# Attention kernel: the score maxima of later units dealt out to the steps by a plan made at build time

## The chip, the cores and the metric

The kernel runs on one core of a Trainium2 chip. The metric is the device time of one execution in microseconds; lower is better. The times of before come from three runs, and one further execution was profiled.

## The reference

Four layers with residuals on 4096 rows of 256 numbers: attention a, a soft mixture of experts, attention b, the same mixture again. Only the attentions matter here. Each has 16 heads of 16 columns and is causal:

```
x = x + attention_a(layernorm(x))       # has a bias bo and a term exp(denom_bias) in the denominator
x = x + experts(layernorm(x))
x = x + attention_b(layernorm(x))
x = x + experts(layernorm(x))

sim  = q @ k^T / 4 per head, masked above the diagonal
e    = exp(sim - max(sim, axis=-1))
attn = e / (sum(e) + exp(denom_bias));  out = (attn @ v) @ Wo^T + bo
```

The row maximum of all scores has to be known before the first exponential of that row.

## The kernel before

**Units and steps.** The queries are cut into 8 blocks of 512 rows, the heads into 4 groups of 4. A unit is one group g of one block b; the 32 units run in the order of `units`, block by block. Two passes are made over a unit's keys.

The first pass, `steps_a(u)`, finds the row maxima. It is a generator, and each of its turns is called a piece here: TensorE writes scores (queries as weights) into two PSUM banks called `bank`, and VectorE takes one maximum from each bank (L410; near the diagonal L431, L444 and L454). A unit of block b has 8b + 5 pieces, so an attention has 1056. The banks come from `net.bank()`, a ring of three (`at_psa`). After a unit's last piece `finish_a` reduces the maxima to one number a row and head (`ng`, L465), splits and transposes it on VectorE (`nt`, L473), and sends it over DRAM into the tile `qm` (two kinds of DMA on SyncE's queue, L475 and L478). The first piece of a key tile loads the next tile (`load_to`, L374; a query tile at L367), into a ring of 11 key tiles and 4 query tiles.

The second pass, `steps_b(u)`, has 4(b + 1) steps for a unit, one for each 128 keys; 576 for an attention. A step has two halves (two heads each): score matmuls (`sc<-q,k`), matmuls that subtract the maxima (`sc<-qm,one`, they need `qm`), and an exponential on ScalarE (L533). The last four steps of a unit lie on the diagonal and are 512, 384, 256 and 128 columns wide; GpSimd masks them (L537). A step's product with the values, `weigh` (`o<-pb,va`), is made one step later. After a unit's last one ScalarE copies `o` (L501) and `epilogue` begins.

**What else is put into the steps.** `net.beside(2)` is called once in each step, between two portions of its pieces: it counts two, starts what has become due, and then runs one item, of `urgent` first, else of `side`. In blocks 0 to 3 `side` holds the 16 items of `pieces(b + 4)`, begun with the block's first step: two with transposes (items 3 and 8), four projections to queries and keys (10 to 13: four matmuls into a `bank`, a copy on ScalarE L173, a subtraction on VectorE L174, DMAs to DRAM) and two projections to values (14 and 15). The epilogue's parts fall due 6, 8, 4 and 8 counts after one another: the denominators' reciprocal on VectorE (L558, L559), the division on GpSimd (L571), the fetch of the block's output, and two output projections (`project`, added to x on VectorE at L601), which are `urgent`.

**The order.** Every matmul is kept in program order, so the loop at the end of `run` sets TensorE's order: in each step the two halves' scores, then half of the step's pieces, then `beside`, then the values' product of the step before, then the other pieces. How many pieces a step gets is asked of `wanted(n)`, n counting half steps: unit u's pieces lie evenly between the due time of unit u - 1's pieces and its own, and they are due 8 half steps (10 early on) before the unit's second pass begins:

```
due = [0] + [max(0, e - (10 if e <= 32 else 8)) for e in ends[:-1]]
...
return first + -(-(ends_a[u] - first) * (n - lo) // (hi - lo))
```

In the profile, `bank`, `sc` and `o` are TensorE's outputs, all recorded at the helper's line L68.

Of the kernel before, what the change touches and what calls it, by code (L numbers as in the profile page):

```python
# [24 lines left out]
NQB = S // QB  # L25
# [3 lines left out]
NG = H // HG  # L29
# [14 lines left out]
class _Net:  # L44
# [28 lines left out]
    def bank(self):  # L73
        return self.banks.tile([P, 512], F32, name="bank")
# [32 lines left out]
class _Attention:  # L107
# [158 lines left out]
    def dense_values(self, b, psb=None):  # L266
        bank = (lambda: self.front(psb)) if psb else self.net.bank
        return [lambda t2=t2: self.values(b, t2, bank()) for t2 in range(2)]

    def run(self, ready, experts):  # L270

# [4 lines left out]
        with ExitStack() as ctx:  # L276
# [13 lines left out]
            before = [cp.tile([P, P], F32R, name=f"before{n}") for n in range(2)]  # L290
            behind = cp.tile([P, half], F32R, name="behind")
            for n in range(3):
                w = P if n < 2 else half
                f = net.ep.tile([P, QB], F32, name="ot", bufs=3)[:, 0:w]
                for h2 in range(2):
# [3 lines left out]
                        out=fh, in_=fh, compare_op=ALU.is_ge, fill=1.0 if n < 2 else NEG,  # L299
# [12 lines left out]
            for p in range(2):  # L312
                f = net.ep.tile([P, QB], F32, name="ot", bufs=3)[:, 0:P]
                nc.gpsimd.memset(f, 0.0)
                for h2 in range(2):
                    for l in range(2):
                        nc.gpsimd.affine_select(
                            out=f, in_=f, compare_op=ALU.not_equal, fill=1.0,
# [28 lines left out]
            pairs = deque([psb])  # L347

            def third():
                actx.close()  # L350
                pairs.extend([psb, pool("psc", 1, space=PSUM)])
                net.banks = pool("psx", 1, space=PSUM)

            ks, qs, qms = {}, {}, {}
            units = [(g, b) for b in range(NQB) for g in range(NG)]


            kseq = [(u, kb) for u, (g, b) in enumerate(units) for kb in range(b + 1)]
# [145 lines left out]
            def values_to(n):  # L504
                while len(queue) > n:
                    weigh(queue.popleft())
# [99 lines left out]

            ends, ends_a, total = [], [], 0
            for g, b in units:  # L610
                ends.append(8 * (b + 1) + (ends[-1] if ends else 0))
                total += 8 * b + 5
                ends_a.append(total)

            due = [0] + [max(0, e - (10 if e <= 32 else 8)) for e in ends[:-1]]
            runs = iter(f for u in range(len(units)) for f in steps_a(u))
            done_a = [0]

            def maxima_to(n):
                while done_a[0] < min(n, total):  # L620
                    next(runs)
                    done_a[0] += 1

            def wanted(n):
                for u in range(len(units)):
                    if due[u] > n:
                        lo, hi = due[u - 1], due[u]
                        first = ends_a[u - 1]
                        return first + -(-(ends_a[u] - first) * (n - lo) // (hi - lo))
                return total  # L630

            front = []
            if ready:
# [15 lines left out]
                front += self.dense(b, psb, prp)  # L649
            for f in front:  # L650
                f()
                maxima_to(min(done_a[0] + 1, wanted(0)))
            maxima_to(wanted(0))
            n = 0
            for u, (g, b) in enumerate(units):
                if g == 0 and 4 <= b + 4 < NQB:
                    net.side.extend(self.pieces(b + 4))
                if g == 0 and b == NQB - 1:
                    experts.load()

                last = deque()
                if u == len(units) - 1:
                    last.extend(experts.ahead())
                    third()
                for p, _ in enumerate(steps_b(u)):
                    n += 1
                    if last and p % 4 == 3 and p >= 8 * (b + 1) - 4 * len(last):
                        last.popleft()()
                    if p % 2 == 0:
                        continue  # L670
                    while (
                        g >= 2 and net.side and u + 2 < len(units)
                        and units[u + 2][1] > max(3, b)
                    ):
                        net.beside()
                    want = wanted(n + 1)
                    maxima_to((done_a[0] + want) // 2)
                    net.beside(2)
                    values_to(1)
                    maxima_to(want)  # L680
# [622 lines left out]
```

## Time and profile before

| | us |
|---|---|
| median of three runs (5069.66 to 5073.91) | 5070.28 |
| the profiled execution, and its span | 5074.49, 5072.8 |
| first attention's steps, in the span | 86.2 to 1753.7 |
| second attention's steps | 2619.1 to 4289.3 |
| TensorE busy, share of the span | 4938.9, 97% |
| VectorE busy | 4087.2, 81% |
| ScalarE busy | 2631.4, 52% |

In a line of the timeline stand the start, the time, the engine, the line of the code, the operation with its tiles and shapes, how many instructions were merged (x2), and in brackets the engine's idle time before them and what ended it. In a group's line stand the count, the busy time and the mean in ns of one, and after the second bar the engine's idle time just before them. In a line of the stages stand the stretch, its length, the busy time of TensorE, its weight loads, VectorE, ScalarE and GpSimd with the number of instructions, the granted TensorE clock, and the DMA engines' share and rate. A line of the waits names who waited for whom: total us, times, longest.

### The profile page before, as it was taken

Reading aid. Unit: us, or ns where it says so; the run is one execution under the profiler, and the core shown is the slowest. Engines: PE = TensorE matmul, PEld = TensorE weight load, DVE = VectorE, ACT = ScalarE, POOL = GpSimd, SP = SyncE. Lnnn points to the kernel's source line nnn. Section 1 sums busy time; section 2 is a strip of 40 time slices with the busy share of each in tenths; the row PEclk is TensorE's granted clock in tenths of the full one; section 3 lists DMA queues with packets and bytes.
Section 4 is the critical chain, followed back from the end, with each engine's and each line's share of the span. In section 5 each row is a group of like instructions: output and inputs, shape, how many; then the busy total and the mean of one; then the engine's idle time right before and its main releaser. Section 6 shows DMA issues by size and latency. Waiting matters only on the chain.

```text
span 5072.8 us, 79746 instructions
## 1 busy us (share of the span) xinstructions
PE 4938.9 (97%) x31216; PEld 2706.8 (53%) x31216; DVE 4087.2 (81%) x6392; ACT 2631.4 (52%) x3112; POOL 1175.7 (23%) x1178
## 2 busy tenths in 40 slices
PE   7999999999999999999989999999999999999999
PEld 4555455555455444458855555555554554444588
DVE  5688989898988378887757888898989883888877
ACT  4566666766667721223235666667666677212222
POOL 3211100000000155554422111000000001555454
PEclk9999999999999999999999999999999999999999
DMA  7433222221111013443454332222211210134443
GB/s 261 147 113 126 76 67 70 65 67 63 57 63 57 33 73 113 146 143 122 147 186 147 115 126 75 66 70 62 70 63 58 63 57 33 75 113 146 144 146 111
DMA packets 266442, 499.20 MB, mean 98 GB/s; under 512 B 44976, under 2 KB 110000, under 8 KB 258384
## 3 DMA queue, kind: packets, MB, share of 16 engines
q1 hardware_dynamic: 260832, 485.57, 28.8%
q10 hardware_dynamic: 4896, 7.87, 0.5%
q8 instruction: 245, 4.01, 0.3%
q14 instruction: 133, 1.09, 0.1%
q0 software_dynamic: 336, 0.66, 0.0%
HBM read 336.73 MB, written 156.76 MB: 97 GB/s over the span
## 4 chain that ended last, share of the span: by engine, by line
PE 86%; DVE 8%; DMA 2%; ACT 2%; issue 1%; POOL 1%; SPq 0%; ACTq 0%; POOLq 0%; DVEq 0%
PE o L68 27%; PE bank L68 21%; PE sc L68 18%; PE acc L68 9%; PE lg L68 8%; DVE mx L410 4%; PE ps L71 2%; ACT pb L533 1%; PE bank L71 0%; DVE lT L1013 0%; DVE mx L454 0%; DMA d<-ot 0%; DMA rb<-dd 0%; ACT L533 0%; DMA l<-ld 0%
## 5 line engine op out<-in xcount | busy, mean ns | idle before, releaser
L533 ACT ACTIVATE pb<-sc 128x1024 f32<-128x1024 f32 (+3 forms) x2304 | 2070.1, 951 | 1080.4 <-PE sc L68 1077.6
L410 DVE TENSOR_REDUCE mx<-bank 128x1 f32<-128x512 f32 x3584 | 2223.2, 682 | 236.6 <-PE bank L68 231.3
L68 PE MATMUL bank<-k,q 64*128 64x512 f32 (+3 forms) x5376 | 1222.3, 413 | 50.8 <-DVE mx L410 23.3
L68 PEld LDWEIGHTS bank<-k,q 64*128 64x128 f32 x5376 | 659.1, 185 | 1022.8 <-DVE mx L410 735.1
L68 PE MATMUL o<-pb,va 128*32 128x512 f32 (+3 forms) x9216 | 1154.2, 571 | 1.6 <-ACT ot L501 1.3
L68 PE MATMUL sc<-q,k 64*128 64x512 f32 (+3 forms) x4608 | 941.6, 386 | 11.2 <-ACT pb L533 11.1
L68 PE MATMUL sc<-qm,one 64*128 64x512 f32 (+3 forms) x4608 | 915.4, 376 | 0.0
L68 PEld LDWEIGHTS sc<-q,k 64*128 64x128 f32 x4608 | 477.7, 186 | 138.0 <-issue 50.9
L68 PEld LDWEIGHTS sc<-qm,one 64*128 64x128 f32 x4608 | 488.7, 186 | 71.5
L757 ACT ACTIVATE e<-e 128x1024 f32<-128x1024 f32 x126 | 133.3, 1058 | 651.9 <-POOL e L756 651.9
L68 PE MATMUL acc<-e,x 128*128 128x512 f32 x1008 | 461.7, 602 | 9.1 <-POOL e L764 9.1
L68 PE MATMUL o<-ys,lT 128*128 128x256 f32 x2048 | 459.0, 381 | 0.0
L68 PE MATMUL lg<-zone,xnT 128*128 128x512 f32 x1008 | 453.1, 592 | 1.2 <-ACT xnT L1036 1.2
L68 PEld LDWEIGHTS o<-ys,lT 128*128 128x128 f32 x2048 | 385.4, 191 | 56.7 <-issue 7.0
L537 POOL TENSOR_SCALAR_AFFINE_SELECT pb<-pb 128x256 f32<-128x256 f32 x512 | 204.8, 406 | 839.3 <-ACT pb L533 832.3
L68 PEld LDWEIGHTS o<-pb,va 128*32 128x32 f32 x9216 | 183.1, 108 | 312.3 <-issue 282.4
L955 POOL TENSOR_TENSOR e<-l,mc 128x1024 f32<-128x1024 f32 x120 | 281.2, 2365 | 284.6 <-DMA l<-ld 186.8
L756 POOL TENSOR_TENSOR e<-l,m 128x1024 f32<-128x1024 f32 x126 | 240.9, 1912 | 423.7 <-DVE m L755 419.2
L68 PEld LDWEIGHTS acc<-e,x 128*128 128x128 f32 x1008 | 190.5, 192 | 245.4 <-issue 229.8
L388 POOL MEMSET mx<- 128x192 f32 x64 | 16.3, 259 | 1312.0 <-DVE ng L465 1292.3
L68 PEld LDWEIGHTS lg<-zone,xnT 128*128 128x128 f32 x1008 | 190.3, 190 | 234.3 <-issue 223.8
L741 DVE TENSOR_TENSOR l<-lg,zone 128x512 f32<-128x512 f32 x252 | 173.0, 690 | 135.8 <-PE lg L68 131.0
(145 smaller groups left out, 3675.5 us busy)
## 6 DMA issues: line engine op xcount, KB each, us to landing
k<-ak SPq DMA_DIRECT2D x144, 512.0 KB
k<-bk SPq DMA_DIRECT2D x144, 512.0 KB
ld<-l SPq DMA_DIRECT2D x126, 512.0 KB
l<-ld SPq DMA_DIRECT2D x60, 1024.0 KB
w<-in_L_ffn_expert_w_dram SPq DMA_DIRECT2D x26, 1024.0 KB
q<-aq SPq DMA_DIRECT2D x32, 512.0 KB
rb<-dd SPq DMA_DIRECT2D x64, 256.0 KB
q<-bq SPq DMA_DIRECT2D x32, 512.0 KB
```

The source lines that it names most:

```text
L68: self.tc.keep_in_program_order(self.nc.tensor.matmul(*a, **k))
L71: self.tc.keep_in_program_order(self.nc.tensor.transpose(o, i, self.ident))
L388: nc.gpsimd.memset(mx, -3e38)
L410: nc.vector.tensor_reduce(flat[:, o : o + 1], scs[h2], AX.X, ALU.max)
L533: nc.scalar.activation(pb[:, :, off:QB], sc[:, :, off:QB], AF.Exp)
L537: nc.gpsimd.affine_select(out=d, in_=d, compare_op=ALU.is_ge, fill=0.0, base=0, pattern=[[0, 2], [1, P]], channel_multiplier=-1,)
L741: pin(net.nc.vector.tensor_tensor(l, lg, self.phb[:, ds(h * (E // 2) + n * 512, 512)], ALU.add))
L756: pin(nc.gpsimd.tensor_tensor(e3, l3, _bc(m.unsqueeze(2), [P, ne, SLOT]), ALU.subtract))
L757: nc.scalar.activation(e, e, AF.Exp)
L955: pin(nc.gpsimd.tensor_tensor(e[:, ns, :], l, _bc(cms[t].unsqueeze(1), [P, NH, SLOT]), ALU.subtract))
```

## The change

`wanted` and the due times go. In their place the new `plan` fixes, before the loop, how many pieces are done after each of the 576 steps; the loop reads `plan[n]`. The plan gives each step a time for TensorE (`pe`) and one for VectorE (`dve`) from fixed numbers, with additions where it takes the items of `side` and the output projections to be, and a time on VectorE for 0 to 5 pieces (`pairs`). Among all ways to deal the pieces it chooses the one whose steps' larger times have the least sum. Its bounds: the pieces of a unit are done four steps before the unit begins (`late`), and the pieces run no further ahead than the rings of 11 key tiles and 4 query tiles allow (`ahead`, `held`). The pieces themselves, their order and what a step does are the same; before the first step 10 pieces are done, as before.

```diff
+    @staticmethod
+    def plan(units, kseq, first_of, ends_a, at_start):
+        rows, ahead, held, late = 4, 11, 4, 4
+        steps = [(u, kt) for u, (g, b) in enumerate(units) for kt in range(4 * (b + 1))]
+        part = lambda u, kt: min(4, 4 * (units[u][1] + 1) - kt) / 4
+        pe, dve = [], []
+        before = 0
+        for u, kt in steps:
+            w = part(u, kt)
+            pe.append(0.33 + 0.93 * w + 0.86 * before)
+            dve.append(0.05)
+            before = w
+        for b in range(NQB):
+            s = first_of[NG * b]
+            if b:
+                for n in (11, 12):
+                    pe[s + n] += 2.1
+                    dve[s + n] += 0.9
+            if b + 4 < NQB:
+                for n in (3, 8):
+                    pe[s + n] += 0.6
+                for n in range(10, 16):
+                    pe[s + n + 2 * (b > 0)] += 1.8
+                    dve[s + n + 2 * (b > 0)] += 0.7 * (n < 14)
+        pairs = (0, 1.25, 2.39, 3.89, 5.1, 6.3)
...
+        for s, (u, kt) in enumerate(steps):
+            least.append(max([e for v, e in enumerate(ends_a) if first_of[v] <= s + late] + [0]))
+            cap = 0
+            while cap < ends_a[-1]:
+                k = tile_of[cap]
+                last = kseq[min(k + 1, len(kseq) - 1)][0]
+                if k + 2 - tiles[u] - kt // rows > ahead or last > u + held - 1:
+                    break
+                cap += 1
+            most.append(max(cap, least[-1]))
+        best, back = {at_start: 0.0}, []
+        for s in range(len(steps)):
+            new, came = {}, {}
+            for done, cost in best.items():
+                for n in range(len(pairs)):
+                    to = done + n
+                    if not least[s] <= to <= most[s] and not (n == 0 and to > most[s]):
+                        continue
+                    c = cost + max(pe[s] + 0.25 * n, dve[s] + pairs[n], 2.7 * (n == 2) * (pe[s] > 2))
...
-            due = [0] + [max(0, e - (10 if e <= 32 else 8)) for e in ends[:-1]]
...
-            def wanted(n):
-                for u in range(len(units)):
-                    if due[u] > n:
-                        lo, hi = due[u - 1], due[u]
-                        first = ends_a[u - 1]
-                        return first + -(-(ends_a[u] - first) * (n - lo) // (hi - lo))
-                return total
+            at_start = ends_a[1]
+            plan = self.plan(units, kseq, first_of, ends_a, at_start)
...
-                    want = wanted(n + 1)
+                    want = plan[n]
+                    n += 1
                     maxima_to((done_a[0] + want) // 2)
                     net.beside(2)
                     values_to(1)
```

## The prediction

> **What bounds the kernel now.** I read the chain of the page first, then the costliest groups, then the waits.
>
> ```profile
> PE 86%; DVE 8%; DMA 2%; ACT 2%; issue 1%; POOL 1%; SPq 0%; ACTq 0%; POOLq 0%; DVEq 0%
> L410 DVE TENSOR_REDUCE mx<-bank 128x1 f32<-128x512 f32 x3584 | 2223.2, 682 | 236.6 <-PE bank L68 231.3
> L68 PEld LDWEIGHTS bank<-k,q 64*128 64x128 f32 x5376 | 659.1, 185 | 1022.8 <-DVE mx L410 735.1
> PEld bank L68 <- DVE mx L410: 783.5, 1253, 1.7
> ```
>
> TensorE carries the chain, but 8% of it lies on VectorE, and the weight load of a maxima matmul waits 783.5 us in all for a VectorE reduction to give back a bank. So the time of one step has to be read, by how many pieces of maxima were dealt to it. ScalarE runs two exponentials in each step, so the distance of two rows of its timeline is one step. Ordinary steps, and one with three pieces:
>
> ```profile
> 1351.66 1.94 ACT L533 ACTIVATE pb<-sc 128x1024 f32<-128x1024 f32 x2 [0.77 <-PE sc L68]
> 1354.37 1.94 ACT L533 ACTIVATE pb<-sc 128x1024 f32<-128x1024 f32 x2 [0.77 <-PE sc L68]
> 1357.06 1.94 ACT L533 ACTIVATE pb<-sc 128x1024 f32<-128x1024 f32 x2 [0.76 <-PE sc L68]
> 1361.04 1.94 ACT L533 ACTIVATE pb<-sc 128x1024 f32<-128x1024 f32 x2 [2.04 <-PE sc L68]
> 1363.66 1.02 ACT L533 ACTIVATE pb<-sc 128x1024 f32<-128x1024 f32 x1 [0.69 <-PE sc L68]
> ...
> 1530.58 1.94 ACT L533 ACTIVATE pb<-sc 128x1024 f32<-128x1024 f32 x2 [0.77 <-PE sc L68]
> 1532.95 1.94 ACT L533 ACTIVATE pb<-sc 128x1024 f32<-128x1024 f32 x2 [0.43 <-PE sc L68]
> ```
>
> Two pieces: 2.70 us. Three pieces: 1357.06 to 1363.66 is 6.60 for two steps, 1.20 more than 5.40. One piece: 2.37. None (the last unit, rows at 1691.04 and 1693.17): 2.13. So a first piece costs 0.24, TensorE's own time; a second 0.34; a third 1.20, two reductions of 0.6 that TensorE waits for, because three banks hold one piece and a half. The end of a unit, with two pieces in each step, and below it one with a single piece in the quarter-wide step:
>
> ```profile
> 1509.56 1.09 ACT L533 ACTIVATE pb<-sc 128x512 f32<-128x512 f32 x2 [1.08 <-PE sc L68]
> 1511.98 0.66 ACT L533 ACTIVATE pb<-sc 128x256 f32<-128x256 f32 x2 [1.33 <-PE sc L68]
> 1514.74 1.94 ACT L533 ACTIVATE pb<-sc 128x1024 f32<-128x1024 f32 x2 [2.10 <-PE sc L68]
> ...
> 343.84 0.66 ACT L533 ACTIVATE pb<-sc 128x256 f32<-128x256 f32 x2 [1.34 <-PE sc L68]
> 345.54 1.94 ACT L533 ACTIVATE pb<-sc 128x1024 f32<-128x1024 f32 x2 [1.05 <-PE sc L68]
> ```
>
> The narrow steps have little TensorE work, so VectorE sets them: 2.76 with two pieces, 1.70 with one, a saving of 1.0 (0.05 comes back in the next step). In the half-wide step it is 0.80 (2.49 and 1.69 between first score matmuls). That is what a plan can earn. A step with a projection of the next queries, keys or values (a "work" step below) is the other place:
>
> ```profile
> 453.34 0.69 DVE L174 TENSOR_TENSOR zone<-bank,zone 128x512 fp32r<-128x512 f32 x1 [1.00 <-ACT zone L173]
> 454.21 2.48 DVE L410 TENSOR_REDUCE mx<-bank 128x1 f32<-128x512 f32 x4 [0.18 <-PE bank L68]
> 458.19 0.69 DVE L174 TENSOR_TENSOR zone<-bank,zone 128x512 fp32r<-128x512 f32 x1 [1.50 <-ACT zone L173]
> 459.00 1.29 DVE L410 TENSOR_REDUCE mx<-bank 128x1 f32<-128x512 f32 x2
> ```
>
> VectorE idles 1.0 to 1.5 us beside the projection's matmuls, yet only because nothing is queued for it: the projection's result holds the third bank until L174 has read it (matmuls from 455.56, read until 458.88).
>
> **The change, part by part.** No instruction is added or removed: 1056 pieces an attention, each with its matmuls, two reductions and key loads, move between steps. Both rules are integer arithmetic, so I worked each through for the 576 steps and counted. "Second +39" means that 39 more steps have a second piece.
>
> Ordinary full-width steps: first +2, second +39, third -8: 0.5 + 39 x 0.34 - 8 x 1.20 = +4.2 us. Three-quarter-wide: second +1, third -3: 0.3 - 3.6 = -3.3. Half-wide: second -22, third -2: -22 x 0.80 - 2 x 1.06 (3.55 against 2.49) = -19.7. Quarter-wide: second -22, third -2: -22 x 1.0 - 2 x 1.07 (3.34 against 2.27) = -24.1. First step of a unit: second -17, third -4. A second piece is nearly free here: first and second step take 5.16 with 1 and 2 pieces, 5.21 with 2 and 2, as the copy of o on ScalarE (L501) is waited for. -17 x 0.05 - 4 x 1.20 = -5.7. Steps with transposes: second +3, third and fourth -1 each: 3 x 0.65 (2.94 to 3.59) - 2.4 = -0.5. Work steps: second +8 at 0.53 (4.26 to 4.79) = +4.2; third and fourth +23 at y. Steps with the output projection: second +2 at 0.53 = +1.1; third +4 at y.
>
> The counts cancel to zero, as they must. Without y the sum is -43.8 us an attention. The plan's own weights put the output projection at a block's steps 11 and 12; it runs at 13 and 14 (counts of 6, 8, 4 and 8, two a step). So in blocks 4 to 7 two third pieces land on ordinary steps; these are the 8 that remain above.
>
> y decides, and no row shows three pieces beside a projection at full clock. From below, a piece costs TensorE's 0.24, if VectorE's idle time takes the reductions. From above the nearest row is the third piece of an ordinary step, 1.20. I take 1.20: pieces go one after another through three banks, one of which the projection holds, so a third piece behind it cannot start its second matmul before the first reduction behind L174 has ended (459.7), where the next step's scores now start at 458.80. 27 x 1.20 = +32.4, or +6.5 at the lower end.
>
> The Trainium skill speaks against the change here: "Perfetto Trace Analysis", Optimization Strategy, says that the same gap coming back on the engine that should be saturated can mean that the next tile has no room in PSUM. By it y is the full wait and the sum is the one with 1.20.
>
> The deadline moves too. In block 7 a unit's last piece now comes four steps ahead of the unit instead of six. From the end of that step the transposed maxima are ready 2.54 us later (unit 31: 1672.48 to 1675.02), the two DMAs (L475, L478) are issued 2.6 later and land some 1.4 after that, as L478 itself waits 1.4 for L475: 6.5 us. Three steps of 2.70, 1.69 and 1.39 and the first scores, 0.23, make 6.0, so units 28 to 30 wait 0.5 each; unit 31, behind steps without pieces (1.99, 1.60, 1.17, 0.34), waits 1.4. Who waits is TensorE at the first sum with qm, with all scores behind it. +2.9. In the other blocks the lead is four to fifteen steps and the waits hide.
>
> On SP's queue the key loads (L374), the maxima's DMAs and the epilogue's keep their order; a load is issued at least two steps after the tile it replaces was used (before: none at the tightest). I cost this at nothing; two steps, 5.4 us, cover it, and if they did not, TensorE would wait for k at 2 to 3 us a tile. GpSimd's memset of mx (L388) moves along; its buffer was given back a unit earlier, so it holds nothing up.
>
> Sum: -43.8 + 32.4 + 2.9 = -8.5 us an attention (blocks 4 to 7: -16.2, blocks 0 to 3: +7.7), -17 for the two. The profiled execution took 5074.49 us (span 5072.8 and 1.7 around it), 4.2 above the median; the sum is a difference, so I take it from the median: 5070.3 - 17 = 5053.
>
> **Rivals.** First, the projections hide the extra reductions: y = 0.24: -34.4 an attention, -69: 5001. For it is the idle VectorE; against it the held bank. Chance 0.07.
>
> Second, the gain is given back on ScalarE. With one piece in the narrow steps, the exponentials and the copy of o become the limit, as in the last unit without pieces, whose half-wide step to second full step takes 5.31 (1679.46 to 1684.77) against 7.57 with two pieces each. I expect 5.72; 0.4 lost at some 19 unit starts would be 7.6 of the 8.5: -2, 5068, no change that can be told. Chance 0.20.
>
> Third, and slower: VectorE stands behind a late denominator. The reciprocal's instructions (L558, L559) are queued among the reductions three steps after d is fetched. In block 1 of both attentions this already fails:
>
> ```profile
> 157.85 0.23 DVE L558 TENSOR_SCALAR d<-d,edb 128x16 f32<-128x16 f32 x1 [6.51 <-DMA d<-ot]
> 150.00:157.00 7.00, 3.55 (x31) 1.94 (x28) 1.29 (x2) 3.88 (x4) 1.27 (x1) 1.00 0.30 76
> 160.00:164.00 4.00, 4.00 (x20) 1.58 (x12) 2.46 (x5) 0.58 (x1) 0.00 (x0) 0.50 0.17 63
> ```
>
> VectorE idles 6.51, TensorE's banks run out (5.4 idle), and its granted clock then stands at 0.50: that step is 7.1 long of an ordinary one and the next 1.2, 8.3 us. The plan takes six pieces out of the first three units, so these get shorter by up to 7 us and a reciprocal comes sooner after its fetch. The rival decides from one more such stall an attention; with two more it is -8.5 + 16.6 = +8.1, +16: 5086. Against it: units 3 and 5 get longer, which may as well remove the stall that is there. Chance 0.19.
>
> The skill's "TensorE: Matmul & The Clock Gate", HAM oscillation, puts the fall of the clock at TensorE gaps over some 3.4 us. By it the waits for qm, 0.5 to 1.4 us, cost only themselves; were each followed by 3.4 us at half clock, the estimate for them would be 2.9 + 4 x 1.7 = 9.7 and the sum -3.
>
> Last, the plan does not deal quite as counted, because the pieces in the traced kernel lie a step off: half to two thirds of the gain stay; chance 0.04, taken as -12, 5058.
>
> **The numbers.** About 0.2%, 10 us, is what can be told from no change. The forecast, with y from 0.9 to 1.4 (5037 to 5064), has 0.50: 0.44 of it below 5060, 0.06 within 10 us. Faster: 0.44 + 0.07 + 0.04 = 0.55. Same: 0.06 + 0.20 = 0.26. Slower: 0.19. For 8 in 10 I leave out the case of hidden reductions and the far half of the slow case: 5028 to 5083.
>
> **What would show it.** Right: exponentials 1.7 apart at unit ends; work steps of 6.0 us with three pieces and 7.2 with four; block 4 to the end of the attention (611.4 to 1753.7 here) shorter by 16, the blocks before it longer by 8. Wrong: work steps near 5 us with three pieces; ScalarE never idle from a narrow step to the next unit's second step; more waits of L558 for d.

## The result, and the profile after

| | before | change |
|---|---|---|
| median of 11 runs, us | 5073.91 (5069.48 to 5078.31) | 5086.1 (5079.87 to 5091.3) |
| ratio, 95% interval | | 1.0024 (1.0016 to 1.0032) |
| profiled execution, span, us | 5074.49, 5072.8 | 5085.1, 5083.0 |
| first, second attention's steps, us | 1667.5, 1670.2 | 1675.5, 1674.2 |

The change makes the kernel slower by 12 us, 0.24%. I forecast 17 us less (5053, from the 5070.3 of the first three runs). The page of the changed kernel, which answers to the three lines of before (chain, groups, waits; the code has moved down by 64 lines, so L410 is L474 now):

```profile
PE 84%; DVE 8%; ACT 3%; DMA 2%; issue 2%; POOL 1%; SPq 0%; ACTq 0%; POOLq 0%; DVEq 0%
L474 DVE TENSOR_REDUCE mx<-bank 128x1 f32<-128x512 f32 x3584 | 2234.7, 683 | 276.9 <-PE bank L68 266.8
L68 PEld LDWEIGHTS bank<-k,q 64*128 64x128 f32 x5376 | 641.7, 185 | 1012.8 <-DVE mx L474 708.6
PEld bank L68 <- DVE mx L474: 767.7, 1103, 2.5
```

The wait for a bank fell by 16 us only (783.5 to 767.7), while VectorE idles 40 us more in front of its reductions (236.6 to 276.9). TensorE waits a little less for VectorE, and VectorE more for TensorE.

**Where it went.** The time of each block of units, against before, in both attentions, beside what the prediction's prices give:

| us an attention | forecast | first | second |
|---|---|---|---|
| blocks 0 to 3 | +7.7 | +15.8 | +13.3 |
| blocks 4 to 6 | -21.0 | -17.2 | -19.8 |
| block 7 | +4.8 | +9.4 | +10.5 |
| sum | -8.5 | +8.0 | +3.9 |

So the gain at the ends of units came nearly as forecast, and two losses are each about twice as large. The end of a unit on ScalarE's timeline, as shown for before:

```profile
1344.25 1.09 ACT L597 ACTIVATE pb<-sc 128x512 f32<-128x512 f32 x2 [1.07 <-PE sc L68]
1345.86 0.66 ACT L597 ACTIVATE pb<-sc 128x256 f32<-128x256 f32 x2 [0.53 <-POOL pb L601]
1347.57 1.94 ACT L597 ACTIVATE pb<-sc 128x1024 f32<-128x1024 f32 x2 [1.05 <-PE sc L68]
1349.40 0.59 ACT L565 COPY ot<-o 128x512 f32<-128x512 f32 x1
1349.87 1.05 ACT L597 ACTIVATE pb<-sc 128x1024 f32<-128x1024 f32 x1
```

1.61 and 1.71 apart, where before had 2.42 and 2.76 with two pieces in each.

**Block 7.** The same place one unit later, where block 7 begins; then VectorE's timeline just ahead of it, and the stages around the wait (columns as in the front part):

```profile
1418.28 1.08 ACT L597 ACTIVATE pb<-sc 128x512 f32<-128x512 f32 x2 [1.23 <-PE sc L68]
1419.90 0.66 ACT L597 ACTIVATE pb<-sc 128x256 f32<-128x256 f32 x2 [0.54 <-POOL pb L601]
1423.77 1.94 ACT L597 ACTIVATE pb<-sc 128x1024 f32<-128x1024 f32 x2 [3.21 <-PE sc L68]
```

```profile
1416.45 0.35 DVE L529 TENSOR_REDUCE ng<-mx 128x16 f32<-128x192 f32 x1
1416.72 0.68 DVE L474 TENSOR_REDUCE mx<-bank 128x1 f32<-128x512 f32 x1
1417.31 0.30 DVE L534 CAST nr<-ng 128x16 fp32r<-128x16 f32 x1
1417.53 0.68 DVE L474 TENSOR_REDUCE mx<-bank 128x1 f32<-128x512 f32 x1
1418.13 0.16 DVE L535 TENSOR_TENSOR nr<-ng,nr 128x16 f32<-128x16 f32 x1
1418.21 0.68 DVE L474 TENSOR_REDUCE mx<-bank 128x1 f32<-128x512 f32 x1
1418.81 0.20 DVE L537 STREAM_TRANSPOSE nt<-nr 128x32 f32<-128x32 f32 x1
```

```profile
1420.90:1422.60 1.70, 0.42 (x5) 0.06 (x1) 1.34 (x3) 0.00 (x0) 0.22 (x1) 1.00 0.03 10
1422.80:1426.20 3.40, 3.40 (x20) 1.99 (x21) 0.33 (x1) 2.42 (x3) 0.00 (x0) 0.50 0.83 302
```

Between the small steps that make a unit's maxima ready (L529 to L537) stand reductions of the next unit, whose pieces already run. TensorE has nothing to do for 1.28 us ahead of 1422.55, the first sum with `qm`; then its granted clock is 0.50 for 3.4 us. In block 7 all eight units of the two attentions wait so (1.10 to 1.32 us, the last unit of each attention 0.93), and the half clock follows five times. In the waits of the first attention's steps:

```profile
PE sc L68 <- DMA qm<-md: 4.6, 4, 1.3
```

**A work step.** A step of block 2 that runs a projection to values and has four pieces, 344.32 to 351.51. VectorE's timeline, then TensorE's:

```profile
343.57 4.88 DVE L474 TENSOR_REDUCE mx<-bank 128x1 f32<-128x512 f32 x8 [2.32 <-PE bank L68]
350.77 2.48 DVE L474 TENSOR_REDUCE mx<-bank 128x1 f32<-128x512 f32 x4 [2.32 <-PE bank L68]
```

```profile
345.35 1.86 PE L68 MATMUL bank<-k,q 64*128 64x512 f32 x4
347.31 1.99 PE L68 MATMUL bank<-zone 128*128 128x256 f32 x8
349.23 1.06 PE L68 MATMUL o<-pb,va 128*32 128x512 f32 x8
350.23 0.73 PE L68 MATMUL bank<-k,q 64*128 64x512 f32 x3
351.51 0.50 PE L68 MATMUL bank<-k,q 64*128 64x512 f32 x1 [0.56 <-DVE mx L474]
```

The step is as long as VectorE's eight reductions, 4.88, and the 2.32 in which it waits for TensorE, which then runs the projection and the values' product. In front of these and behind them it is TensorE that waits for VectorE.

The medians over all work steps: two pieces 4.57 (half of them from 4.39 to 4.81), three 5.93, four 7.67; steps with an output projection 4.80 with two, 6.21 with three.

### The profile page after: what moved, and what is told of

Read it like the earlier page. It is cut to its first block, busy times and chain, and to the rows that moved or that the text cites. A ratio compares the mean times of both kernels' runs of the same rounds, so it can differ in the third digit from the quotient of the medians.

```text
span 5083.0 us, 79761 instructions
## 1 busy us (share of the span) xinstructions
PE 4912.9 (97%) x31216; PEld 2706.4 (53%) x31216; DVE 4090.3 (80%) x6392; ACT 2630.3 (52%) x3112; POOL 1174.2 (23%) x1178
## 4 chain that ended last, share of the span: by engine, by line
PE 84%; DVE 8%; ACT 3%; DMA 2%; issue 2%; POOL 1%; SPq 0%; ACTq 0%; POOLq 0%; DVEq 0%
PE o L68 27%; PE bank L68 20%; PE sc L68 18%; PE acc L68 8%; PE lg L68 8%; DVE mx L474 3%; ACT pb L597 2%; PE ps L71 2%; DVE mx L518 1%; DMA rb<-dd 1%; DMA d<-ot 1%; DVE lT L1070 0%; PE bank L71 0%; DVE mx L508 0%; DMA md<-nt 0%
## 5 line engine op out<-in xcount | busy, mean ns | idle before, releaser
L474 DVE TENSOR_REDUCE mx<-bank 128x1 f32<-128x512 f32 x3584 | 2234.7, 683 | 276.9 <-PE bank L68 266.8
L68 PE MATMUL bank<-k,q 64*128 64x512 f32 (+3 forms) x5376 | 1168.4, 412 | 60.4 <-DVE mx L474 35.9
L68 PEld LDWEIGHTS bank<-k,q 64*128 64x128 f32 x5376 | 641.7, 185 | 1012.8 <-DVE mx L474 708.6
L635 POOL TENSOR_TENSOR rb<-ot,rb 128x512 f32<-128x512 f32 x64 | 82.1, 1283 | 773.6 <-DMA rb<-dd 386.4
```

Source lines behind the costliest of these rows:

```text
L68: self.tc.keep_in_program_order(self.nc.tensor.matmul(*a, **k))
L474: nc.vector.tensor_reduce(flat[:, o : o + 1], scs[h2], AX.X, ALU.max)
L635: nc.gpsimd.tensor_tensor(on, ot, on, ALU.mult)
```

## The experiments

All are compared with the kernel before, run along with them. "The change" is the kernel predicted. Times of blocks are of the profiled executions, against before, first/second attention.

**1. The deadline alone**: six steps ahead, in block 7 only.

```diff
-                e for v, e in enumerate(ends_a) if first_of[v] <= s + late
+                e for v, e in enumerate(ends_a)
+                if first_of[v] <= s + (6 if units[v][1] == NQB - 1 else late)
```

> The changed kernel with one bound of the plan moved: the pieces of block 7's units are done six steps ahead of the unit instead of four. Theory A (late maxima): in the changed kernel units 28 to 31 of each attention wait 1.2 to 1.3 us for qm, and the granted clock stands at 0.50 for 3.4 us behind most of these waits (five of eight), 1.7 us each; with VectorE's interleaved chain that is some 8 us an attention. Expected: no wait of TensorE for qm, no half clock at these four unit starts, block 7 at 334 to 335 us instead of 342.6, and the median at about 5070, where the kernel before stands (5074). Theory B (the waits cost what the prediction gave them, 2.9 us an attention, and the half clock would have come anyway): 5080, with half clock still somewhere in block 7.

Measured: 5069.51, ratio 0.9982 (0.9973 to 0.9991). Block 7 +0.2/+1.6 in place of +9.4/+10.5; no wait for `qm` and no half clock in it. So the deadline costs the change 9 us an attention, not 2.9 (the pieces that the edit moves are worth 0.4 by the prediction's prices). The quarter-wide step and the next unit's first are 1.71 apart here, 3.87 in the change (ScalarE's timeline of this kernel):

```profile
1423.04 0.66 ACT L600 ACTIVATE pb<-sc 128x256 f32<-128x256 f32 x2 [0.53 <-POOL pb L604]
1424.75 1.94 ACT L600 ACTIVATE pb<-sc 128x1024 f32<-128x1024 f32 x2 [1.05 <-PE sc L68]
```

**2. The weights of the work steps alone**: in the plan the time of projections stands outside the larger of the two engines' times, at the steps at which they really run, so that the plan no longer takes VectorE to work beside them.

```diff
-                    c = cost + max(pe[s] + 0.25 * n, dve[s] + pairs[n], 2.7 * (n == 2) * (pe[s] > 2))
+                    c = cost + more[s] + max(pe[s] + 0.25 * n, dve[s] + pairs[n], 2.7 * (n == 2) * (pe[s] > 2))
...
-                for n in (11, 12):
-                    pe[s + n] += 2.1
-                    dve[s + n] += 0.9
+                for n in (13, 14):
+                    more[s + n] += 2.1
```

> The changed kernel with other weights in the plan: the time of projections and transposes is added outside of the larger of the two engines' times (so the plan no longer believes that they hide reductions), at the steps where they run (10 to 12 and 15 to 17, the output projection at 13 and 14). The plan then deals no step a third piece. The deadline of four steps stays. Theory A (third and fourth pieces beside a projection cost VectorE's full time, 1.1 to 1.7 us each as the changed kernel's steps show): by the prices of the prediction the sum falls from -9.6 to -36.8 us an attention against the kernel before, less 9 us of late maxima: about 5074 - 56 = 5018, with blocks 0 to 3 of each attention 5 to 15 us below the kernel before. Theory B (pieces beside projections are cheap and the early blocks are slow for another reason, such as key loads that run far ahead): 5075 to 5085, blocks 0 to 3 as in the changed kernel.

Measured: 5032.85, ratio 0.9908 (0.9895 to 0.9922). The plan now deals no step more than two pieces. Blocks 1 to 3 give -21.0/-16.6 in place of +8.8/+8.4; block 7 still loses 8.8/8.6 to its deadline. So theory A holds for these blocks; of the 56 us that it forecast for the whole, 45 came. The edit does two things, it prices the items apart and it puts them at the steps where they run, and what each is worth was not measured.

**3. Both edits.**

> Both edits together: projections priced apart and a deadline of six steps in block 7. Theory A: -33 us an attention by the prices and no wait for qm: 5008; the two effects add, so this is faster than the second by 8 to 16 us less what the earlier deadline costs in narrow steps (3.6 an attention). Theory B: 5070 to 5080.

Measured: 5012.34, ratio 0.9869 (0.9855 to 0.9882): the attentions are 32.0 and 33.0 shorter. The prediction's own prices, put on this dealing, give some 33. This agreement is in part luck: they give -4.5 for block 0, which got longer by 4.0/0.2, and -3.2 for block 1, which got shorter by 11.9/8.4. This version beats both kernels.

**4. The plan from block 4 on**, the even rule before it, deadline as in 1.

```diff
+            if s < len(even):
+                least[-1] = most[-1] = even[s]
```

> Blocks 0 to 3 are dealt evenly as before; from block 4 on the changed kernel's plan, unaltered but for a deadline of six steps in block 7. No step with a projection of pieces() gets more than before. Theory A (the narrow steps earn what was forecast, the loss lies in blocks 0 to 3 and in block 7's deadline): -15 us an attention, 5044 (blocks 4 to 6 shorter by 5 to 7 each, block 7 by 0 to 2). If the gain in the narrow steps were given back on ScalarE: 5070 and more.

Measured: 5057.71, ratio 0.9959 (0.9947 to 0.9972). Blocks 0 to 3 are back to +1.5/+0.3, so what they lose lies in their own dealing. Blocks 4 to 7 give -11.6/-12.0 and the attentions -10.1/-11.6, less than expected. In the change blocks 0 to 3 do 11 pieces more than by the even rule, and here blocks 4 to 7 keep those; but the prediction's prices, put on this dealing with those pieces counted, give the expected -15.0. The shortfall is largest in block 5 (-2.0/-1.9, -5.3 by the prices), and its cause stays open.

**5. The bank given back early**: L174 reads ScalarE's copy in place of the bank (the projections' low part is left out), so the bank is free as soon as ScalarE has copied it.

```diff
-        nc.vector.tensor_tensor(lo.bitcast(F32R), ps, hi, ALU.subtract)
+        nc.vector.tensor_tensor(lo.bitcast(F32R), hi, hi, ALU.subtract)
```

> The changed kernel, leaving out the low part of the split keys and queries in the steps of pieces(): the subtraction (L174) takes the copy from itself instead of reading the bank, so that ScalarE's copy is the bank's last reader. All instructions stay, on the same queues. Theory H (as the prediction put it, the projection's held bank makes a third piece dear): the bank comes free 0.7 us earlier, and the steps with a projection to keys or queries and three or four pieces get shorter by 0.5 to 0.8 (step 11 of block 1: 5.73 to about 5.1; step 12 with four pieces: 7.79 to about 7.1). Theory P (VectorE's pace: three banks hold a piece and a half, so the second matmul of each further piece waits for a reduction, whoever held the third bank): the same steps within 0.2.

Measured: one run, 5083.12. Over all work steps the medians are 5.94 against 5.93 with three pieces and 7.67 against 7.67 with four, but half of these steps project values and have no L174. The steps with a projection to keys or queries decide. Behind block 0 there are six in an attention with three or four pieces. Four did not move, among them the two named above (5.73 and 5.73, 7.79 and 7.80). Two in block 2 got shorter by 0.59 (7.72 to 7.13, 6.58 to 5.99), as theory H has it; the steps behind these got longer by 0.3 to 0.4, and the twelve steps around them take 61.2 and 61.6 in place of 61.7 and 62.2. So the held bank, with which I argued for y = 1.20, is the reason in few steps, and it is worth some 0.5 us an attention there.

**6. Reductions half as long**: over 256 of 512 columns; half of each maximum's scores are left out.

```diff
-                                    flat[:, o : o + 1], scs[h2], AX.X, ALU.max
+                                    flat[:, o : o + 1], scs[h2][:, 0 : QB // 2], AX.X, ALU.max
```

> The changed kernel, leaving out half of each row maximum away from the diagonal: L474's reductions read 256 of the 512 columns. TensorE's work, the banks and the dealing are the same; a reduction should take some 0.4 instead of 0.68. Theory P: a third or fourth piece beside a projection costs little more than TensorE's 0.24 to 0.5 (steps with three pieces 5.9 to about 5.2, with four 7.2 to 7.8 to about 5.8), ordinary steps with three pieces go from 3.65 to about 3.0, blocks 0 to 3 of an attention lose 15 to 25 us. Against it (the third piece is dear through banks or the order alone): steps with three pieces stay over 5.7.

Measured: one run, 4955.88. A reduction takes 419 ns in place of 683. Ordinary steps with two pieces fall from 2.71 to 2.59, with three from 3.77 to 3.42, work steps with four from 7.67 to 6.75, with three from 5.93 to 5.73. A four-piece step has eight reductions, so 2.1 us of VectorE's time are gone and 0.9 us come out. So VectorE's pace is a part of the price, but not the whole of it.

**7. The spread of pieces in TensorE's order** (with the deadline of 1): where a step has three or four, one of the later ones stands between the item and the values' product.

```diff
+                    more = want - done_a[0] > 2
                     maxima_to((done_a[0] + want) // 2)
                     net.beside(2)
+                    if more:
+                        maxima_to(want - 1)
                     values_to(1)
                     maxima_to(want)
```

> The change with the deadline of six steps in block 7, and in a step of three or more pieces one of the later pieces stands between the item and the values' product (one, item, one, values, one; or two, item, one, values, one) instead of all behind the values' product. Theory O (the third and fourth piece cost a full wait because pieces stand next to one another in TensorE's order, while VectorE idles beside the item's and the values' matmuls): work steps with three pieces fall from 5.9 to 5.0-5.3 us, with four from 7.7 to 6.5-6.8, output projections with three from 6.2 to 5.3; about 17 us an attention, 5035 us, ratio 0.991. Theory P (each piece beyond two costs VectorE's own time wherever it stands): steps unchanged within 0.2 us, 5069 us, ratio 0.998.

Measured: 5050.43, ratio 0.9947 (0.9931 to 0.9964), against 0.9982 in experiment 1, from which only the order differs. Work steps with three pieces 5.37, with four 6.98, output projections with three 5.65: 0.56 to 0.70 less each. With 9, 7 and 4 of them an attention that makes 12 us; the attentions are 11 and 11 shorter than in 1. The step shown above, in this kernel (VectorE, then TensorE):

```profile
335.55 4.49 DVE L477 TENSOR_REDUCE mx<-bank 128x1 f32<-128x512 f32 x7
341.37 2.71 DVE L477 TENSOR_REDUCE mx<-bank 128x1 f32<-128x512 f32 x4 [1.32 <-PE bank L68]
```

```profile
338.90 1.99 PE L68 MATMUL bank<-zone 128*128 128x256 f32 x8
340.82 0.50 PE L68 MATMUL bank<-k,q 64*128 64x512 f32 x2
341.26 1.07 PE L68 MATMUL o<-pb,va 128*32 128x512 f32 x8
```

VectorE gets its next banks 1.32 us after its last, not 2.32, and the step is 6.42 long in place of 7.19. So the place of the pieces in the order makes up a good part of what they cost: 0.56 of the 1.14 of a third piece, 0.70 of the 2.88 of a third and a fourth (prices below). Ordinary steps with three pieces, which have no item, gained nothing from the same spread: 3.90 against 3.77. Some two thirds of the fall I expected came; where there are four pieces, two still stand together ahead of the item, which may be a reason and was not tested.

**8. The deadline at five steps** in block 7 (edit as in 1).

> The changed kernel with the deadline in block 7 at five steps instead of four (six was the first experiment). By the times in the changed kernel's trace the maxima come 1.3 us late with four steps, and a fifth adds an ordinary step of 2.70: no wait for qm, no half clock behind a unit start of block 7, block 7 at 334 to 335 us, median about as with six steps, 5069. If the first experiment's gain came from pieces that moved and not from the waits, block 7 lies between 334 and 343.

Measured: 5078.42, ratio 0.9998 (0.9989 to 1.0007). No wait for `qm`; block 7 +1.7/+2.9, so 7.7 an attention better than the change, which is the 13 us between 1.0024 and 0.9998 within the intervals. The time of 5069 did not come. Five steps are enough to hide the chain. A caution comes with it: blocks 0 to 2, dealt alike in the change and in 1 and 8, sum to +22, +22 and +33 us over the two attentions. So these blocks can differ by some 10 us with the same dealing; where that comes from was not settled, and a difference of that size in them shows nothing.

**9. Before, with the short deadline**: the even rule, block 7's pieces due about four steps ahead.

```diff
-                max(0, e - (10 if e <= 32 else 8))
+                max(0, e - (10 if e <= 32 else 8 if units[v + 1][1] < NQB - 1 else 5))
```

> The kernel before with its even dealing, block 7's due times moved so that the last piece comes four steps ahead of the unit, as in the changed kernel. Its narrow steps keep two pieces and last 2.5 to 2.8 us instead of 1.4 to 1.7, so the same four steps are some 1.7 us longer. If the waits of the changed kernel come from the narrow steps that the plan has made short, TensorE waits for qm only at unit 31 (no pieces behind it; 1 to 2 us) and 0 to 0.4 at units 28 to 30: 5074 to 5082. If four steps are too few whatever they hold: waits of 1.3 at all four and half clock behind them, 5088 to 5094.

Measured: 5075.59, ratio 0.9993 (0.9984 to 1.0002). The maxima of units 28 to 30 become ready just as late after the start of the unit before's three-quarter-wide step (4.08 us, as in the change), but the three narrow steps take 7.84 with two pieces each and 5.94 with fewer: no wait, 0.45 us to spare. Only unit 31, behind steps without pieces, waits 0.9. So the lead of four steps is harmful because the same plan made those steps short.

**10. A later denominator** (with both edits of 3): the reciprocal due one step later.

```diff
-                net.after(6, invert)
+                net.after(8, invert)
-                    net.after(8, divide)
+                    net.after(6, divide)
```

> The projections' time apart and the deadline of six steps, and the denominators' reciprocal due one step later (8 counts after the copy of o, the division then 6 after it, so that it stays where it was). Theory D (in block 0 VectorE still stands behind a late denominator, and eight times in all for 24.1 us): VectorE's waits for d fall below 8 us, the third step of unit 3 (8.41 and 12.00) falls to about 5.3, blocks 0 to 2 together by 6 to 12 us in the two attentions, 5000-5006 us against 5012, ratio 0.985. Theory E (the wait moves on: GpSimd's division waits for rb and the masks behind it): GpSimd's waits for rb rise by as much, time within 4 us of 5012.

Measured: 5009.1, ratio 0.9863 (0.9848 to 0.9877), not to be told from experiment 3. VectorE's waits for d are 40.6 us against 43.3, and the third step of unit 3 takes 8.55 and 9.59 against 8.41 and 12.00. The theory falls: one step more does not free VectorE of it.

## Why the prediction was wrong

An attention was forecast at -8.5 and came out at +8.0 and +3.9, so 16.5 and 12.4 us are missing: 8.1 and 5.6 in blocks 0 to 3, 4.6 and 5.7 in block 7, 3.8 and 1.2 in blocks 4 to 6. Two terms of the sum failed: the deadline's +2.9, which measured 9, and the +7.7 of blocks 0 to 3, which measured 15.8 and 13.3.

**The ends of units: right.** Narrow steps cost what the rows of before said (1.68 and 1.39 with one piece); blocks 4 to 6 gave 17 to 20 of 21 us.

**The deadline: the mechanism right, its size wrong.** "From the end of that step the transposed maxima are ready 2.54 us later (unit 31 ...)". I took it from unit 31, behind which no pieces are queued. For units 28 to 30 of the change it is 4.08 (once 3.95), since three reductions of the next unit stand between the small steps on VectorE. In before these units show 2.54 to 2.57, with none or one in between, so no row of before had the larger number: it comes with the later place, in experiment 9 too. The rest of the chain held: the issues take 2.59 and the data is usable 0.93 after. 4.08 + 2.59 + 0.93 = 7.6, against 6.17 to the first sum, up to which TensorE still has the first scores: it idles 1.1 to 1.3, not 0.5 (unit 31: 0.9, forecast 1.4). Then the half clock, which I set aside: five of eight times, 3.4 us each, in which by my estimate 1.7 us of work are lost: 4 us an attention. Forecast 2.9, measured 9 (experiment 1). The prediction did name this case, at 9.7; but its sum is then -8.5 + 6.8 = -1.7 an attention (the -3 there fits the two together), so even with it a small gain was forecast. Without the deadline's loss the change is at 0.9982: faster by 0.18%, about the least that can be told.

**y, the third and fourth piece of a work step: about right in size, mostly wrong in cause.** Forecast 1.20; measured 1.14 for a third (5.93 less the 4.79 that I had priced two at), 1.74 for a fourth, 1.41 beside an output projection (6.21 less 4.80), about 36 an attention in place of 32.4. But the cause that I gave, "a third piece behind it cannot start its second matmul before the first reduction behind L174 has ended", shows in only two of six such steps in experiment 5, and the step shown above has no L174 at all. So the size was in part luck. Experiment 7 shows a larger cause: TensorE's matmuls stand in program order, pieces stand together before the item and behind the values' product, and there they are paid at VectorE's pace while the item's 2 and the product's 1 us pass with VectorE idle. One piece put between the two took back 0.56 to 0.70 a step, shorter reductions (experiment 6) 0.20 with three pieces and 0.92 with four; what makes up the rest was not taken apart. The idle time I saw beside the projections in before is real, but a piece must stand there in the order to use it.

**Blocks 0 to 3: the sum was short by 6 to 8 us.** With the measured y it would be some +11.3, of +15.8/+13.3. What is left is mainly block 0, where I forecast -0.2 and it lost 7.0/4.9, less what block 1 did better than its prices (+3.3 forecast, -0.4/-1.8 measured). The prices of single pieces do not hold in these short steps; I take it that they wait for many things at once. One of these waits in the profile of the change, VectorE's timeline and its sum of waits for d:

```profile
139.40 0.23 DVE L622 TENSOR_SCALAR d<-d,edb 128x16 f32<-128x16 f32 x1 [3.43 <-DMA d<-ot]
```

```profile
  DMA d<-ot: 43.8, 21
```

The stall of before at 157.85 is gone (its steps take 2.71 now) and this one has come in unit 3 of block 0, whose second step takes 8.28 and 8.38. Experiment 4 shows that the dealing of blocks 0 to 3 does it; which of the waits in block 0 ends last was not settled (experiment 10 moved one and won nothing), so the cause of this part stays open.

**The rivals.** Hidden reductions (5001): refuted, y is over 1. ScalarE (5068): from the half-wide step to the next unit's second full step it takes 5.6 (rows at 1344.25 and 1349.87), where 5.72 was forecast without any loss; refuted. The late denominator named the time that came, 5086 (+16 forecast, +12 measured), but by luck: VectorE's waits for d fell from 49.4 to 43.8 in all, though there are 21 in place of 17. A plan that deals otherwise: it dealt as counted.

## What to carry to other kernels

Adding up an engine's free time in a step says little of whether work can use it: where an engine's order is fixed, as TensorE's is here, the gap that helps is the one that an extra piece stands in (experiment 7), so a planner should price the place, not the sum. Between the change and experiment 2 a plain surcharge, at the right steps, in place of the larger of two sums was worth 59 us. A deadline counted in steps must be checked again when the same edit makes those steps shorter, and its chain must be timed where other work is queued between its links. A price read at one place of a trace need not hold where the change moves the work, here 2.54 against 4.08.

## What was not expected of the hardware

TensorE's granted clock fell behind gaps much shorter than I had allowed for. In the change and experiments 2 and 5, 24 waits for `qm` in block 7 left TensorE idle for 0.93 to 1.47 us. Behind the six of 0.93 to 1.04 the clock stayed at 1.00; behind 11 of the 18 of 1.10 to 1.47 it stood at 0.50 within 2 us, for 3.4 us, once for 6.8.

What tells the 11 from the other seven can be read from the records of the granted clock. In every run here all its changes within the run lie on one grid of 3.41 us (in the change half clock begins at 1422.78, 1518.35, 1607.10, 3962.29 and 4057.87 in block 7, always whole steps of the grid apart). Twelve of the 18 longer gaps lie within one step of this grid, and half clock follows 11 of them with the next step; six are cut in two by an edge of it, and none of these is followed by half clock. One gap of each kind in the change, by steps of the grid: 1.32 us whole within the first row, and 1.25 us cut at 4143.21.

```profile
4054.45:4057.87 3.42, 2.10 (x20) 1.01 (x16) 1.29 (x2) 0.86 (x1) 0.16 (x1) 1.00 0.42 109
4057.87:4061.28 3.41, 3.41 (x16) 1.53 (x18) 1.89 (x3) 3.41 (x5) 0.00 (x0) 0.50 0.15 52
4139.79:4143.21 3.42, 2.77 (x30) 1.16 (x22) 3.23 (x7) 1.50 (x4) 1.58 (x4) 1.00 0.03 5
4143.21:4146.62 3.41, 2.76 (x20) 1.30 (x20) 1.08 (x3) 1.86 (x3) 0.00 (x0) 1.00 0.60 158
4146.62:4150.03 3.41, 3.28 (x26) 1.78 (x26) 2.86 (x7) 2.72 (x5) 0.00 (x0) 1.00 0.02 2
```

This is no full rule: outside block 7 there are steps of the grid with 1.4 us of idle time in all that are followed by full clock.

The Trainium skill's "TensorE: Matmul & The Clock Gate", HAM oscillation, which the prediction used, asks for gaps over some 3.4 us; these rows disagree, and they decide. The same page (What's actually happening) says that the window in which activity is counted runs freely; the grid agrees with that.
